# Two interleaved passes on one core: the rows, counts and rounds of the neighbour skipping take other places, and some operands move from SBUF to PSUM

## The chip, the cores and the metric

One Trainium2 chip, of which the program uses one core. A core has TensorE (matmuls and transposes, written to PSUM), VectorE (DVE), ScalarE (ACT), GpSimd (POOL) and SyncE (SP, which here only issues DMAs). Each works through its own queue in order and waits for the others by semaphores. The metric is the device time of one execution in microseconds, median of several runs.

## The reference, cut to what matters

Two layers on 16 graphs of 1024 nodes with 128 features and a 0/1 adjacency. Layer 0 is a gated graph network of four steps, then a residual and a normalization. Layer 1 first thins out the adjacency (the "skipping"), row after row, and then runs three aggregation layers on it.

```python
# layer 0, four steps
hw = einsum('bnc,cd->bnd', h, weight[i]);  m = einsum('bjn,bjd->bnd', adj, hw)
h = gru_cell(m, h, w_ih[i], w_hh[i], b_ih[i], b_hh[i])
...
# layer 1, the skipping: one step for each row n, in order
row = take(carry, n);  num = sum(row)
sf = where(num > 10, (num + 1) // 2, 1)
rank = cumsum(row)
rm = row & (rank % sf == 0)          # and only if num > 1 and the node is valid
carry[n] = row & ~rm;  carry[:, n] &= ~rm
```

A removal in a row also takes the entry out of that column, so later rows depend on earlier ones.

## The kernel before, in words

The program has two parts. The first, which the change touches, runs two passes side by side: class `Gated` (layer 0) and class `FixPoint` (the skipping). The second, `sage_layers`, is not touched. The order on every engine of the first part is the order in which the code issues instructions: nothing is reordered there, except in the preparation of the weights ahead of it.

**Gated.** Two streams, each with one graph at a time, take turns: for each pair of graphs and each step l from 0 to 3, one layer for stream 0 (s=0, called layer A here), then one for stream 1 (layer B). A layer is `layer(st, l, aside)`. Its 32 matmuls L1024 multiply the node features by the adjacency. The features are split into `h_hi` (rounded) and `h_lo` (the rest), and each part takes 16 matmuls over eight blocks `h_a` of the adjacency. Two ScalarE copies (L1029) bring the result to `h_ms`. Then come, for each half f of the nodes, six gate matmuls L1038 into the three `h_g` buffers, with a sigmoid (L1047), two VectorE operations (L1049, L1051), a tanh (L1052), a second sigmoid (L1055), and the new state: `h_zh` on GpSimd (L1057), `h_r` on VectorE (L1058), `h_h` on GpSimd (L1059).

While one stream computes, the other is made ready in callbacks `aside(n)`: `next_layer(f)` transposes the new state (L978, into the single PSUM buffer `h_tr`) and splits it; ScalarE writes `h_hi` (L968) and a copy `h_w` (L970), and GpSimd subtracts to get `h_lo` (L971). Around l=0, when a graph ends, `finish` adds the result to `h_x` and stores it to `e_sum` (L1010), `load_x` and `load_adj` load the next graph, `begin_rows` splits its features and `begin` transposes them (L990) into the state. Loads of `h_x` and stores of `e_sum` are issued by SP, loads of `h_a` by POOL.

**FixPoint.** A round treats rows k*128 to k*128+127 of G=4 graphs; k goes from 0 to 7 for each group of four graphs, so there are 32 rounds. The generator `steps` has 20 pieces for a round, each ended by `yield`. `aside` takes one piece at each call, and one more at the end of a layer, so a round lasts two layers, ten pieces in each. Layers A of a round have s=0, and since there are four steps l, rounds with k=0 and k=4 have l=0.

A round has these steps. `turn(i, g)` transposes the removals of earlier rows into the single PSUM buffer `f_tr` (L725, from `f_rt`, read back from memory, and from `f_nr`, the rows of the round before). `count` multiplies them into the row block `f_a` (L732) and scans it to `f_rank`, the running count (L734). `params` makes the divisors `f_q` (L699 to L703). `diag_u` (ScalarE, L856), `removed` (L863) and `less` (matmuls L871 into `f_pd`) solve the 128 x 128 diagonal block in two rounds of a fixed point; `f_both` (L795) marks the pairs in it that are present in both directions, from `f_low` (GpSimd, L767) and its transpose (L782). `wide_u` (ScalarE, L879 and L882) and the rows `end(g)` (L834) then give the block's removals `f_nr` for all columns; `end(g)` also stores them to `e_nr`, loads the `f_a` that is six row blocks on, and multiplies `f_s` on GpSimd (L840). `end(4)` adds up a check (L828, L830).

Before the change, the pieces stood so: layer A: rows 2 and 3; check; turn and count 0 with turns and counts 1, 2, 3 after them; transposes of `f_low`; `read_back` of the next round's `f_rt`. Layer B: `params`, `f_both`, `removed`, `less`, `removed`, `less`, `wide_u` of four graphs, rows 0 and 1.

Of the kernel before, what the change touches and what calls it, by code (L numbers as in the profile page):

```python
# [630 lines left out]
class FixPoint:  # L631
# [96 lines left out]
    def count(self, i, g, a, rank):  # L728
        nc = self.nc
        k, b0 = self.todo[i]  # L730
        if k:
            nc.vector.tensor_mul(a[:, :k * P], a[:, :k * P], self.pt[:, :k, :].rearrange("p k n -> p (k n)"))  # L732
        start = self.first[:, k, b0 + g:b0 + g + 1]
        nc.vector.tensor_tensor_scan(rank[:, g, 1:N + 1], self.zero.to_broadcast([P, N]), a,  # L734
                                     start, op0=ALU.add, op1=ALU.add)

    def steps(self):

        nc, G = self.nc, self.G
        for c in range(self.LOTS):  # L740
            self.load(c)
        end = None
        for i, (k, b0) in enumerate(self.todo):
            n0 = k * P
            diag = slice(n0, n0 + P)
            after = slice(n0 + 1, n0 + 1 + P)
            a = [self.loaded.pop((i, g)) for g in range(G // 2)]
            rank = self.two.tile([P, G, N + 2], F16, name="f_rank")

            if end:  # L750
                end(2)
                end(3)
            a += [self.loaded.pop((i, g)) for g in range(G // 2, G)]
            yield

            if end:
                end(4)
            nc.vector.tensor_copy(rank[:, :, 0], self.first[:, k, b0:b0 + G])
            yield

            self.turn(i, 0)
            self.count(i, 0, a[0], rank)
            yield
            self.turn(i, 1)
            low = self.small.tile([P, G, P], BF, name="f_low")
            for g in range(G):
                nc.gpsimd.affine_select(low[:, g, :], a[g][:, diag], pattern=[[-1, P]],  # L767
                                        compare_op=ALU.is_gt, fill=0.0, base=0, channel_multiplier=1)
            yield
            self.count(i, 1, a[1], rank)  # L770
            yield
            self.turn(i, 2)
            self.count(i, 2, a[2], rank)
            yield
            yield
            self.turn(i, 3)
            self.count(i, 3, a[3], rank)
            yield

            pt = self.ps.tile([P, G, P], BF, name="f_pd")  # L780
            for g in range(G):
                nc.tensor.transpose(pt[:, g, :], low[:, g, :], self.cst["ident_b"])  # L782
            yield

            for g in range(G):
                self.read_back(i + 1, g)
            yield

            q = self.params(rank[:, :, N])
            u = self.diag_u(rank[:, :, after], q)  # L790
            yield

            both = self.small.tile([P, G, P], BF, name="f_both")
            for g in range(G):
                nc.vector.tensor_mul(both[:, g, :], a[g][:, diag], pt[:, g, :])  # L795
            yield
            x = self.removed(u, q, both)
            yield

            yield  # L800
            rd = self.small.tile([P, G, P], F16, name="f_rd")
            pd, num = self.less(x, rank)
            q = self.params(num)
            nc.vector.tensor_sub(rd, rank[:, :, after], pd)
            u = self.diag_u(rd, q)
            yield

            yield
            x = self.removed(u, q, both)
            yield  # L810

            pd, num = self.less(x, rank)
            q = self.params(num)
            if k + 1 < NB:

                dn = self.small.tile([P, G], F32, name="f_dn")
                nc.vector.tensor_mul(dn, pd[:, :, P - 1], q[:, 0, :])
                nc.vector.tensor_sub(q[:, 3, :], q[:, 1, :], dn)
            nc.vector.tensor_sub(rank[:, :, after], rank[:, :, after], pd)
            us = {}  # L820
            self.wide_u(k, 0, us, rank, q)
            self.wide_u(k, 1, us, rank, q)
            yield
            s = self.small.tile([P, G, P], BF, name="f_s")

            def end(g, i=i, k=k, b0=b0, n0=n0, diag=diag, us=us, q=q, a=a, s=s, x=x, both=both):
                if g == G:
                    nc.gpsimd.tensor_tensor(s, s, x, ALU.add)  # L828
                    junk = self.small.tile([P, G, P], F16, name="f_ud")
                    nc.vector.scalar_tensor_tensor(junk, s, 1.0, both, op0=ALU.mult, op1=ALU.not_equal,  # L830
                                                   accum_out=self.bad[:, i:i + 1])
                    return
                nr = self.wide.tile([P, N], BF, name="f_nr", bufs=5)
                nc.vector.scalar_tensor_tensor(nr, us[g], q[:, 2, g:g + 1], a[g],  # L834
                                               op0=ALU.not_equal, op1=ALU.is_ge)
                nc.sync.dma_start(self.not_r[b0 + g, n0:n0 + P, :], nr)
                self.fresh[g] = nr
                self.load(G * i + g + self.LOTS)

                nc.gpsimd.tensor_tensor(s[:, g, :], nr[:, diag], both[:, g, :], ALU.mult)  # L840


            end(0)
            self.wide_u(k, 2, us, rank, q)
            self.wide_u(k, 3, us, rank, q)
            yield

            end(1)
            yield
        for g in range(2, G + 1):  # L850
            end(g)

    def diag_u(self, rd, q):
        u = self.small.tile([P, self.G, P], F16, name="f_ud")
        for g in range(self.G):
# [31 lines left out]
class Gated:  # L887
# [56 lines left out]
    class Stream:  # L944
# [14 lines left out]
        def load_x(self, b):  # L959
            if b < B:  # L960
                self.x[b] = self.top.wk.tile([P, NB, C], F32, name="h_x", bufs=3)
                self.nc.sync.dma_start(self.x[b], rows_of(self.top.x[b]))

        def split(self, f, src, whole):

            nc = self.nc
            rows = slice(4 * f, 4 * f + 4)
            nc.scalar.copy(self.hi[:, rows, :], src)  # L968
            if whole is not src:
                nc.scalar.copy(whole, src)  # L970
            nc.gpsimd.tensor_tensor(self.lo[:, rows, :], whole, self.hi[:, rows, :].bitcast(F32), ALU.subtract)  # L971

# [8 lines left out]
        def next_layer(self, f):  # L981
            self.split(f, self.turn(f), self.top.wk.tile([P, 4, P], F32, name="h_w"))

# [9 lines left out]
        def begin_rows(self, b):  # L993
            x = self.x[b]
            for f in range(2):
                rows = slice(4 * f, 4 * f + 4)
                self.split(f, x[:, rows, :], x[:, rows, :])

        def finish(self, f):
# [9 lines left out]
            if f == 1:  # L1009
                nc.sync.dma_start(rows_of(self.top.summed[b]), self.x.pop(b))  # L1010

    def layer(self, st, l, aside):
# [5 lines left out]
        for part in (st.hi, st.lo):  # L1018
            for j in range(NB):
                if j % 4 == 0:  # L1020
                    aside(n)
                    n += 1
                for f in range(2):
                    nc.tensor.matmul(pm[f], part[:, j, :], st.adj[j][:, half[f]],  # L1024
# [16 lines left out]
        for f in range(2):  # L1041
# [4 lines left out]
            pr = gate((w(self.wh, 0), h), (w(self.wi, 0), m))  # L1046
            nc.scalar.activation(r, pr, AF.Sigmoid, bias=bias(self.bs, 0))  # L1047
            ph = gate((w(self.wh, 2), h))
            nc.vector.scalar_tensor_tensor(r, ph, bias(self.bh, 2), r, op0=ALU.add, op1=ALU.mult)  # L1049
            px = gate((w(self.wi, 2), m))  # L1050
            nc.vector.tensor_add(r, px, r)  # L1051
            nc.scalar.activation(r, r, AF.Tanh, bias=bias(self.bi, 2))  # L1052
            aside(5 if f == 0 else 7)
            pz = gate((w(self.wh, 1), h), (w(self.wi, 1), m))
# [4 lines left out]
            nc.gpsimd.tensor_tensor(h, zh, r, ALU.subtract)  # L1059
            aside(6 if f == 0 else 8)  # L1060

    def run(self, steps):
# [7 lines left out]
        first.begin_rows(first.b)  # L1070
        for f in range(2):
            first.begin(f)
        for b0 in range(0, B, 2):
# [10 lines left out]
    def beside(self, ot, l, s, b0, steps):  # L1084
# [3 lines left out]
        if before in (0, L0):  # L1088
            old = not (s == 0 and b0 == 0)
            new = not (s == 1 and b0 + 2 >= B)  # L1090
            jobs = {5: [], 6: [], 7: [], 8: []}
            nxt = ot.b + 2 if old else ot.b
# [5 lines left out]
            if old:  # L1098
                jobs[5].append(lambda: ot.finish(0))
                jobs[6].append(lambda: ot.finish(1))  # L1100
                jobs[0] = [lambda: ot.load_x(nxt)]
                for j in range(NB):
                    jobs.setdefault(j // 2, []).append(lambda j=j: ot.load_adj(nxt, j))
            if new:
                jobs.setdefault(3 if old else 0, []).append(lambda: ot.begin_rows(nxt))
                jobs[7].append(begin)
                jobs[8].append(lambda: ot.begin(1))
        else:
            jobs = {5: [lambda: ot.next_layer(0)], 6: [lambda: ot.next_layer(1)]}

        def aside(n):
            next(steps, None)
            for job in jobs.get(n, ()):
                job()
            if n == 8:
                next(steps, None)
        return aside
# [90 lines left out]
```

## Time and profile before

| what | us |
|---|---|
| median of 3 runs (lowest to highest) | 3901.48 (3900.77 to 3902.44) |
| the profiled execution | 3903.16 |
| its span, first to last instruction | 3901.4 |
| VectorE busy in the span | 2743.0 (70%) |
| TensorE busy in the span | 2968.1 (76%) |
| GpSimd busy in the span | 1221.2 (31%) |
| last L834 of the first part starts | 1978.9 |

The page lists busy time by engine, the span in 40 slices, DMA queues, the chain of waits that ended last, the costliest groups of instructions and the DMA issues. In a line of a group or of the timeline, `out<-in` names the tiles; a bracket or the part behind the last bar gives the idle time of the engine ahead of it and what ended that. A duration under `xN` in the timeline spans N instructions.

### The profile page before, as it was taken

What the parts mean: (1) busy time and instruction counts of PE and PEld (TensorE: products, weight loads), DVE (VectorE), ACT (ScalarE), POOL (GpSimd) and SP (SyncE); (2) the same over time, 40 slices, a digit from 0 to 9 for tenths busy, and PEclk for the clock granted to TensorE, in tenths of its full rate; (3) what the DMA queues carried; (4) which work ended last, traced back from release to release, by engine and by line L of the source; (5) the groups of instructions that cost most, each with busy time, mean ns of one, the idle gap of its engine ahead of it and who ended that gap; (6) DMA issues with size and microseconds to landing.
All of it is one profiled execution on the core that took longest, in us unless ns stands there. A gap on an engine that the chain in (4) does not pass through costs nothing. (4 is left out here: it accounts for less than half of the span.)

```text
span 3901.4 us, 29884 instructions
## 1 busy us (share of the span) xinstructions
PE 2968.1 (76%) x9457; PEld 1604.6 (41%) x9457; DVE 2743.0 (70%) x4205; ACT 1149.9 (29%) x2006; POOL 1221.2 (31%) x1031
## 2 busy tenths in 40 slices
PE   5777767777677776767756867778687999899954
PEld 3444434444344443444433434434343444344422
DVE  3776767767677676766768888888885555455688
ACT  2443444434444443444321011010111333222221
POOL 2554455544555455554511001010100222122200
PEclk9898888988888888888877878888788999999976
DMA  4233232322324223242255656565564777576623
GB/s 149 69 118 103 78 135 69 129 93 79 135 69 141 80 79 135 69 159 63 63 174 188 210 172 221 172 211 205 178 209 174 245 240 243 191 243 238 221 76 98
DMA packets 305769, 577.76 MB, mean 148 GB/s; under 512 B 61057, under 2 KB 164258, under 8 KB 305602
## 3 DMA queue, kind: packets, MB, share of 16 engines
q1 hardware_dynamic: 287170, 508.64, 39.2%
q0 software_dynamic: 18432, 67.12, 4.7%
q8 instruction: 77, 1.26, 0.1%
q14 instruction: 90, 0.74, 0.1%
HBM read 449.79 MB, written 125.89 MB: 148 GB/s over the span
## 5 line engine op out<-in xcount | busy, mean ns | idle before, releaser
L455 POOL TENSOR_TENSOR s_os<-s_os,s_mf 128x512 f32<-128x512 f32 x96 | 121.7, 1267 | 1253.3 <-issue 1034.4
L1038 PE MATMUL h_g<-h_ms,h_wi 128*128 128x512 f32 x768 | 405.3, 610 | 120.1 <-ACT h_ms L1029 120.1
L434 PE MATMUL s_a<-b_at,s_t 128*128 128x512 f32 x1024 | 453.4, 593 | 0.0
L1038 PE MATMUL h_g<-h_h,h_wh 128*128 128x512 f32 x768 | 413.5, 621 | 10.4 <-ACT h_r L1047 10.4
L734 DVE TENSOR_TENSOR_SCAN f_rank<-f_zero,f_first,f_a 128x1024 f16<-128x1024 f32 x128 | 325.0, 2541 | 31.3 <-DMA f_a<-in_adj_dram 27.3
L454 DVE RECIPROCAL s_sq<-s_sq 128x512 f32<-128x512 f32 x96 | 321.0, 3344 | 33.4 <-ACT s_sq L453 33.4
L528 PE MATMUL a_pe<-ident,a_a 128*128 128x128 f32 x1024 | 177.6, 324 | 216.8 <-DVE a_a L523 114.8
L1057 POOL TENSOR_TENSOR h_zh<-h_z,h_h 128x512 f32<-128x512 f32 x128 | 250.0, 1953 | 258.2 <-ACT h_z L1055 258.2
L1024 PE MATMUL h_m<-h_a,h_lo 128*128 128x512 f32 x1024 | 325.3, 477 | 0.0
L1058 DVE SCALAR_TENSOR_TENSOR h_r<-h_z,h_r 128x512 f32<-128x512 f32 x128 | 171.0, 1336 | 191.3 <-ACT h_z L1055 191.1
L971 POOL TENSOR_TENSOR h_lo<-h_w,h_hi 128x512 fp32r<-128x512 f32 x96 | 146.4, 1525 | 487.7 <-ACT h_w L970 487.7
L434 PEld LDWEIGHTS s_a<-b_at,s_t 128*128 128x128 f32 x1024 | 195.1, 191 | 246.0 <-issue 245.8
L535 PE MATMUL s_o<-a_at,ones 128*128 128x512 f32 x512 | 265.0, 666 | 21.5 <-DVE a_at L529 21.5
L1038 PEld LDWEIGHTS h_g<-h_ms,h_wi 128*128 128x128 f32 x768 | 149.1, 196 | 316.7 <-issue 170.5
L1049 DVE SCALAR_TENSOR_TENSOR h_r<-h_g,h_bh,h_r 128x512 f32<-128x512 f32 x128 | 95.7, 747 | 260.0 <-PE h_g L1038 170.9
L1024 PE MATMUL h_m<-h_a,h_hi 128*128 128x512 f32 x1024 | 266.2, 414 | 0.0
L528 PEld LDWEIGHTS a_pe<-ident,a_a 128*128 128x128 f32 x1024 | 146.8, 169 | 287.4 <-issue 209.9
L1024 PEld LDWEIGHTS h_m<-h_a,h_lo 128*128 128x128 f32 x1024 | 235.5, 236 | 70.1 <-POOL f_low L767 18.9
L834 DVE SCALAR_TENSOR_TENSOR f_nr<-f_u,f_q,f_a 128x1024 bf16<-128x1024 f16 x128 | 232.0, 1870 | 0.0
L434 PE MATMUL s_a<-a_at,a_s 128*128 128x512 f32 x512 | 230.2, 592 | 0.0
L1024 PEld LDWEIGHTS h_m<-h_a,h_hi 128*128 128x128 f32 x1024 | 195.7, 194 | 50.9 <-issue 11.5
L1059 POOL TENSOR_TENSOR h_h<-h_zh,h_r 128x512 f32<-128x512 f32 x128 | 191.1, 1493 | 31.2 <-DVE f_q L700 23.0
(153 smaller groups left out, 4942.8 us busy)
## 6 DMA issues: line engine op xcount, KB each, us to landing
b_at<-at SPq DMA_DIRECT2D x256, 512.0 KB, 4.4
h_a<-in_adj_dram POOLq DMA_DIRECT2D x128, 512.0 KB, 8.5
f_a<-in_adj_dram SPq DMA_DIRECT2D x128, 512.0 KB, 4.9
a_a<-in_adj_dram SPq DMA_DIRECT2D x128, 512.0 KB, 4.1
at<-a_at SPq DMA_DIRECT2D x32, 2048.0 KB, 8.8
e_nr<-f_nr SPq DMA_DIRECT2D x128, 256.0 KB, 3.7
a_nr<-e_nr SPq DMA_DIRECT2D x32, 1024.0 KB, 7.3
s_mf<-in_nodemask_dram SPq DMA_DIRECT2D x48, 512.0 KB, 4.3
```

The source lines that it names most:

```text
L434: nc.tensor.matmul(pa[f], rows[j // 4][:, j % 4, :], at[j][:, f * HF:(f + 1) * HF], start=(j == 0), stop=(j == NB - 1))
L454: nc.vector.reciprocal(sq, sq)
L528: nc.tensor.transpose(pe[:, i, :], a[:, j * P:(j + 1) * P], ident)
L535: nc.tensor.matmul(pd, ones, at[j][:, f * HF:(f + 1) * HF], start=(j == 0), stop=(j == NB - 1))
L734: nc.vector.tensor_tensor_scan(rank[:, g, 1:N + 1], self.zero.to_broadcast([P, N]), a, start, op0=ALU.add, op1=ALU.add)
L834: nc.vector.scalar_tensor_tensor(nr, us[g], q[:, 2, g:g + 1], a[g], op0=ALU.not_equal, op1=ALU.is_ge)
L971: nc.gpsimd.tensor_tensor(self.lo[:, rows, :], whole, self.hi[:, rows, :].bitcast(F32), ALU.subtract)
L1024: nc.tensor.matmul(pm[f], part[:, j, :], st.adj[j][:, half[f]], start=(j == 0 and part is st.hi), stop=(j == NB - 1 and part is st.lo))
L1038: nc.tensor.matmul(pg, lhs, rhs, start=(i == 0), stop=(i == len(mm) - 1))
L1057: nc.gpsimd.tensor_tensor(zh, z, h, ALU.mult)
L1058: nc.vector.scalar_tensor_tensor(r, z, 1.0, r, op0=ALU.subtract, op1=ALU.mult)
L1059: nc.gpsimd.tensor_tensor(h, zh, r, ALU.subtract)
```

## The change: what it does

*Rows.* `end(0)` to `end(3)` move to the first four pieces of the next round, so to the places between the 32 matmuls of layer A. `wide_u` of the fourth graph follows `end(0)` (`more`). The other three come in the last piece of layer B.

*Counts and turns.* Each turn and each count has a piece of its own: turn and count 0, turn 1, count 1 between the gates of layer A; turn 2, count 2, turn 3 (with `read_back`), count 3 between the 32 matmuls of layer B. The check moves from the second piece to the last of layer A. The solution of the diagonal block follows in layer B from the start of its gates.

*Operands.* The scan takes the row block as first operand and, instead of a column of zeros in SBUF, a column of the PSUM buffer `f_tr`, whose value it ignores (op1 is bypass). `diag_u` writes to PSUM in float32 (name `f_pd`, one buffer, shared with `less` and the diagonals' transposes). The diagonals are transposed in float32 right out of `f_a`, and one GpSimd select on `f_both` takes the place of four on `f_low`. `h_lo` of a next layer is subtracted on VectorE out of `h_tr` (`rest`), without the copy `h_w`; only `begin_rows` still subtracts on GpSimd, from `h_x` itself.

*Places and queues in Gated.* There is a tenth call of `aside`, behind the second half's first sigmoid, so that the places run from 0 to 9, and no double step at the end. `next_layer` and `rest` take places 5 to 8. `begin(1)` moves into the stream's own first layer, ahead of the third of its four groups of matmuls. Loads of `h_x` and stores of `e_sum` are issued by POOL.

```diff
     def count(self, i, g, a, rank):
...
+        out, start = rank[:, g, 1:N + 1], self.first[:, k, b0 + g:b0 + g + 1]
         if k:
...
-        nc.vector.tensor_tensor_scan(rank[:, g, 1:N + 1], self.zero.to_broadcast([P, N]), a,
-                                     start, op0=ALU.add, op1=ALU.add)
+            nc.vector.tensor_tensor_scan(out, a, pt[:, 0, 0:1].to_broadcast([P, N]), start,
+                                         op0=ALU.add, op1=ALU.bypass)
+        else:
+            nc.vector.tensor_tensor_scan(out, a, self.zero.to_broadcast([P, N]), start,
+                                         op0=ALU.add, op1=ALU.add)
...
+            for g in range(G):
+                if end:
+                    end(g)
+                    if g == 0:
+                        more()
+                yield
+            a = [self.loaded.pop((i, g)) for g in range(G)]
             rank = self.two.tile([P, G, N + 2], F16, name="f_rank")
...
             nc.vector.tensor_copy(rank[:, :, 0], self.first[:, k, b0:b0 + G])
+            pt = self.ps.tile([P, G, P], F32, name="f_pd")
+            for g in range(G):
+                nc.tensor.transpose(pt[:, g, :], a[g][:, diag], self.cst["ident"])
             yield
 
             self.turn(i, 0)
             self.count(i, 0, a[0], rank)
             yield
...
             for g in range(G):
                 nc.vector.tensor_mul(both[:, g, :], a[g][:, diag], pt[:, g, :])
+            nc.gpsimd.affine_select(both, both, pattern=[[0, G], [1, P]], compare_op=ALU.is_gt, fill=0.0,
+                                    base=0, channel_multiplier=-1)
+            yield
+            self.turn(i, 1)
+            yield
+            self.count(i, 1, a[1], rank)
+            yield
+            if end:
+                end(G)
+            yield
+            self.turn(i, 2)
+            yield
+            self.count(i, 2, a[2], rank)
+            yield
+            self.turn(i, 3)
+            for g in range(G):
+                self.read_back(i + 1, g)
+            yield
+            self.count(i, 3, a[3], rank)
+            yield
...
     def diag_u(self, rd, q):
-        u = self.small.tile([P, self.G, P], F16, name="f_ud")
+        u = self.ps.tile([P, self.G, P], F32, name="f_pd")
...
-                self.nc.sync.dma_start(self.x[b], rows_of(self.top.x[b]))
+                self.nc.gpsimd.dma_start(self.x[b], rows_of(self.top.x[b]))
...
+    def rest(self, f):
             rows = slice(4 * f, 4 * f + 4)
+            self.nc.vector.tensor_sub(self.lo[:, rows, :], self.src, self.hi[:, rows, :].bitcast(F32))
...
-                nc.sync.dma_start(rows_of(self.top.summed[b]), self.x.pop(b))
+                nc.gpsimd.dma_start(rows_of(self.top.summed[b]), self.x.pop(b))
...
                     aside(n)
                     n += 1
+                    if n == 3 and l == 0:
+                        st.begin(1)
...
+            if f == 1:
+                aside(7)
...
-            aside(5 if f == 0 else 7)
+            aside(5 if f == 0 else 8)
...
-            aside(6 if f == 0 else 8)
+            aside(6 if f == 0 else 9)
...
-            jobs = {5: [lambda: ot.next_layer(0)], 6: [lambda: ot.next_layer(1)]}
+            jobs = {5: [lambda: ot.next_layer(0)], 6: [lambda: ot.rest(0)],
+                    7: [lambda: ot.next_layer(1)], 8: [lambda: ot.rest(1)]}
```

## The prediction

> **What bounds the kernel now.** The page's slices show POOL busy in the first half only: the changed part, "the two passes", is the first 1985 us. The chain of waits holds lines of the later stages only, so I read this part round by round. A round of the skipping is two layers: A (stream 0) and B (stream 1). First the windows answer (us, then busy PE, PEld, DVE, ACT, POOL, then the granted clock): one round from the last L871 of one to that of the next, and the whole steady part.
>
> ```profile
> 1797.40:1853.66 56.26, 44.38 (x161) 26.55 (x160) 42.76 (x62) 23.29 (x40) 27.16 (x21) 0.91 0.21 68
> 112.00:1928.00 1816.00, 1336.31 (x4749) 790.26 (x4750) 1284.81 (x1791) 745.73 (x1331) 920.53 (x781) 0.88 0.31 100
> ```
>
> No engine is full. TensorE has most work and stops in layer A twice each round, and the clock falls after each stop (timeline, PE and DVE):
>
> ```profile
> 1799.93 0.68 DVE L819 TENSOR_TENSOR f_rank<-f_rank,f_pd 128x512 f16<-128x512 f16 x1
> 1804.80 7.23 DVE L834 SCALAR_TENSOR_TENSOR f_nr<-f_u,f_q,f_a 128x1024 bf16<-128x1024 f16 x4
> 1807.14 0.29 PE L725 MATMUL f_tr<-ident_b,f_nr 128*128 128x128 bf16 x1 [3.69 <-DVE f_nr L834]
> 1807.19 3.40 PE L1024 MATMUL h_m<-h_a,h_lo 128*128 128x512 f32 x8
> ...
> 1815.66 0.58 PE L725 MATMUL f_tr<-ident_b,f_rt 128*128 128x128 bf16 x4 [5.07 <-DMA f_a<-in_adj_dram]
> 1832.32 3.91 PE L1024 MATMUL h_m<-h_a,h_hi 128*128 128x512 f32 x16
> ```
>
> The first stop waits for the first new row block f_nr. The second is put down to a DMA long done; the single `f_tr` buffer is what it needs, free at L732 (1814.8), behind four L834 and the L830 junk operation. Eight L1024 then take 3.4 us where sixteen take 3.9. So the round is 41.1 us of matmuls, about 12 of idle TensorE, 3.4 of half clock.
>
> VectorE's own durations are stretched beside GpSimd: four L863 take 1.29 us alone, 4.22 beside L971 and L1057.
>
> ```profile
> 1839.03 1.29 DVE L863 SCALAR_TENSOR_TENSOR f_x<-f_ud,f_q,f_both 128x128 bf16<-128x128 f16 x4
> 1849.51 4.22 DVE L863 SCALAR_TENSOR_TENSOR f_x<-f_ud,f_q,f_both 128x128 bf16<-128x128 f16 x4
> L734 DVE TENSOR_TENSOR_SCAN f_rank<-f_zero,f_first,f_a 128x1024 f16<-128x1024 f32 x128 | 325.0, 2541 | 31.3 <-DMA f_a<-in_adj_dram 27.3
> L971 POOL TENSOR_TENSOR h_lo<-h_w,h_hi 128x512 fp32r<-128x512 f32 x96 | 146.4, 1525 | 487.7 <-ACT h_w L970 487.7
> ```
>
> Rounds are not alike. L758 starts each: 55.2 us apart in rounds with l=1 and 2, 60.2 over l=3, and 70.6 over l=0:
>
> ```profile
> 292.15 0.29 DVE L758 CAST f_rank<-f_first 128x4 f16<-128x4 f32 x1
> 306.82 0.62 ACT L968 CAST h_hi<-h_x 128x512 fp32r<-128x512 f32 x1 [21.21 <-DMA h_x<-in_x_dram]
> 309.84 2.07 PE L1038 MATMUL h_g<-h_ms,h_wi 128*128 128x512 f32 x2 [11.39 <-ACT h_ms L1029]
> 362.79 0.25 DVE L758 CAST f_rank<-f_first 128x4 f16<-128x4 f32 x1
> ```
>
> The load of h_x, issued at 289.4, lands 17 us later behind f_a and h_a; ScalarE waits in order, so h_ms and the gates wait too. This comes seven times. Last, the start:
>
> ```profile
> 35.57 0.90 PE L927 MATMUL h_tr<-ident,h_w_in 128*128 128x128 f32 x3 [28.50 <-DVE h_wi L928]
> ```
>
> A scan (L734) stands ahead of L928 on VectorE and waits for its rows until 32.7; the first L1024 starts at 63.0.
>
> [...]granted 0.50 from 1807 to 1810, after 3.69 us idle. [...]I leave the scan's time as it is when op1 becomes bypass.
>
> **The change, part by part.** Each layer still has ten places. I walk one round (k=5), zero at layer A's first gate matmul, with durations of the trace: gate matmul 0.86, a place of L1024 1.9, turn 0.5, four transposes of h 0.6, count 3.15 (mult 0.8, scan 2.35), PSUM operations of 512 elements 0.7, matmul end to reader 0.27.
>
> *Rows (L834), now in A's first four places, no longer between matmuls.* No L1024 waits for them: the 3.69 and 5.07 us stops go. But the third and fourth row load of the next round are issued after the first and second f_nr, and the new f32 transposes of the diagonals read those rows ahead of A's gates. From B's gates (zero there): L819 ends at 17.2; ScalarE's three f_u follow at 1.43 each; f_nr one 20.2, f_nr two 22.6 (1.22 each, h_h L1059 between). Load issued at 23.05, landing after 3.9 (f_a: 3.3 least, 4.9 median): 27. L1024 ends at about 23.6. TensorE idles some 3 us, and the gates, ScalarE's sigmoid and VectorE's L1049 queue behind it. The f32 transposes take 0.6 for L782's 0.39. The four f_rt loads move to B's third place: they wait on SP for turn 3, ahead of nothing but the next e_nr (16 us later), and are read a layer later: nothing.
>
> *Counts.* The scan now reads one SBUF operand and a PSUM column of `f_tr`, so the next turn waits for the scan, not for the mult. In A: L1051 4.4, count 7.5, L1058 9.1 (held by zh), four `both` 10.0, the new DVE subtraction `rest(0)` 10.7. Only then is `h_tr` free: the second transposes wait 2.2 us. Count 1 ends at 17.1; turn 2, ready at 14.8, waits 2.3. Junk waits for h_h and the f_s sum (1.15), ends at 21.8; count 2 ends at 24.9; turn 3, ready at 21.3, waits 3.6. Count 3 and the parameters end where B's L1024 do.
>
> *`f_ud` to PSUM, one affine for four.* L863 reads one SBUF operand: 1.3 each time, 2.9 less in B. Each of the four activations now waits for the one before: about +0.5, twice. Four POOL selects (1.48) become one of 512 elements (not in the trace: 1.15 from the L828 row to 2.3; off the path, its result is due a layer later). In B the first L871 waits 0.7, the second transposes 2.2 for `rest(0)`.
>
> *Split.* 96 ScalarE copies (0.59) and 96 POOL L971 (1.53) go, 96 DVE subtractions of 0.7 come; counted above.
>
> Sum of a normal round: matmuls 41.4, idle 3.0 + 2.2 + 2.3 + 3.6 + 0.7 + 2.2 + 1.0 = 15.0, half clock after the two gaps over 3 us (1.7 each, at 0.7 chance) 2.4: 58.8, **2.5 us worse** than 56.26. With k=0 there are no turns: 4 us less.
>
> *h_x on POOL's queue.* It is issued behind the first f_s and ahead of h_a; on POOL it stands behind no SP row load. Issue about 22, landing 27 to 29 (h_a's median is 8.5, f_a's 4.9): at most 3 us past the rows, less 1.5 since finish needs no `rest`. Round l=0: +1.5 over normal, against +14.3 now. The e_sum store, too, only follows on POOL. Round l=3: begin(1) leaves the end of B, where L990 waited 4.1 for ScalarE behind f_u, for A's third place: -1 against +4.7.
>
> Eight rounds: k=1,2,5,6 4 x 2.5 = +10; k=3,7 2 x (2.5 - 4.7 - 1) = -6.4; k=4 2.5 - 14.3 + 1.5 = -10.3; k=0 -14.3. Sum -21, four times -84; the first round has no h_x stop (+12.8), the last l=3 no load (+3.7): -67.5.
>
> *Start.* The scan leaves L928's front. All loads of the start (24 of 512 KB, 1.8 MB of weights) are 14.4 MB, 46 us at the 315 GB/s seen while rows load; h_x stands ninth on POOL's queue, the last weights behind six row loads. First L1024 at about 43, between the weights' arrival and the last load: -20 (bounds 0 and -30). *End.* All four f_nr follow the last layer, beside finish: +2.
>
> Sum -85.5 from the profiled execution's 3903.16 us (span 3901.4 and 1.8 around): 3817.7. It lies 1.7 above the median of 3901.48, so I say **3817**. A measurement here can tell 0.2%, 8 us, from no change.
>
> **Rivals.** *Rows land in time:* landing 3.3 and f_nr back to back take away the 3.0 and about 1.0 of half clock in 30 rounds: 3697. For it: L834 of 1.22 between POOL operations; against: 1.5 MB in 4.8 us at 315 GB/s. [...]then 2.9 us stay in B, 30 times 87: 3905, no change. Against: it is short whenever POOL rests. *Slower: the rows in front of the gates.* One mechanism, at the diagonal transposes. Each us of landing costs a us in 30 rounds; it decides from 85.5 / 30 = 2.9 us beyond my 3.9, 6.8 us. At h_a's 8.5 the sum is 30 x 4.6 = +138: 3955. For it: store and load of 0.75 MB per f_nr are queued together; against: f_a's 4.9 median today, with the same stores. *The change does not do what it says* is met by the second case. [...] Slower by 0.2 us, +18.
>
> **How the numbers follow.** Forecast 0.46 (own range 3775 to 3865, from +-1.3 us a round); rows in time or fast scan 0.16; partway between forecast and no change 0.05; no change 0.05; slower 0.28, since a walk leaves out waits more easily than it invents them. Faster 0.66, same 0.06, slower 0.28. The range 3735 to 3925 leaves out one in ten at each end.
>
> **What would show it.** Right: pitch of l=1 rounds near 58, of l=0 near 60; no wait over 5 us of h_hi for h_x; L863 near 0.33 us; new waits of f_pd for f_a (3 us), of f_tr for the scan (2.3 and 3.6), of h_tr for the DVE subtraction (2.2); first L1024 near 43. Wrong: f_pd for f_a above 6.8 us, a granted clock below 0.85, or L834 longer than 1.9.

## The result, and the profile after

The kernel after takes **3915.38 us** (median of 4, 3914.64 to 3915.82), the kernel before 3901.18 beside it: ratio 1.0036, 95% interval 1.0018 to 1.0053. It is slower by about 14 us, where 84 us less were forecast. The profiled execution has a span of 3913.8 us against 3901.4.

Line numbers of the kernel after, where they differ: rows f_nr L833, product L734, scan L736 (L739 for k=0), rank copy L761, transposes of the diagonal L764, removal L858, `less` L866, transposes of h L973, rest L966, adjacency matmuls L1023, gates L1037, h_zh L1058, h_h L1060, h_hi of a new graph L992, load of h_x L957, copies to h_ms L1028.

First the windows answer (columns as before: us, then busy PE, PEld, DVE, ACT, POOL, then the granted clock), for one round from the last L866 of one round to that of the next, and for the steady part. The round has k=6 (its product L734 below runs over 768 columns); the one that the prediction shows of before has k=5:

```profile
399.79:459.12 59.33, 44.22 (x166) 26.09 (x164) 39.95 (x64) 21.52 (x36) 18.27 (x14) 0.94 0.21 67
112.00:1928.00 1816.00, 1372.50 (x4711) 803.88 (x4710) 1155.09 (x1870) 682.50 (x1202) 693.62 (x612) 0.90 0.29 98
```

VectorE, ScalarE and GpSimd all have less to do than before (1155 us for 1285, 682 for 746, 694 for 921), and the clock is no lower. Yet this round is 3 us longer than the round of before in the prediction, which lasts 56.26 us, and 4 us longer than before's mean for k=6 (55.9). Work was taken off engines that were not full; what counts is where TensorE stops. This is the timeline of that round, its stops in layer A:

```profile
404.35 6.50 DVE L833 SCALAR_TENSOR_TENSOR f_nr<-f_u,f_q,f_a 128x1024 bf16<-128x1024 f16 x4 [0.71 <-ACT f_u L877]
413.31 0.33 PE L764 MATMUL f_pd<-ident,f_a 128*128 128x128 f32 x1 [3.12 <-DMA f_a<-in_adj_dram]
425.42 0.63 PE L973 MATMUL h_tr<-ident,h_h 128*128 128x128 f32 x4 [1.97 <-POOL h_h L1060]
431.95 0.44 PE L725 MATMUL f_tr<-ident_b,f_rt 128*128 128x128 bf16 x5 [2.47 <-DVE f_rank L736]
439.70 0.44 PE L725 MATMUL f_tr<-ident_b,f_rt 128*128 128x128 bf16 x5 [3.53 <-DVE f_rank L736]
```

The two stops of before (3.69 for f_nr, 5.07 for `f_tr`) are gone, and four new ones stand there: a late row (3.12), `h_tr` (1.97; put down to h_h, but the h_h that it reads was ready at 407.0, and it starts 0.14 us behind the end of L966, so the buffer is what it needed), and two turns that wait for the scan. These four are close to the forecast's 3.0, 2.2, 2.3 and 3.6. The surprise stands in layer B, all engines in order of time:

```profile
450.79 1.77 POOL L1058 TENSOR_TENSOR h_zh<-h_z,h_h 128x512 f32<-128x512 f32 x1 [15.22 <-ACT h_z L1056]
451.54 1.04 DVE L699 SCALAR_TENSOR_TENSOR f_t<-f_num,f_const 128x4 f32<-128x4 f32 x1
452.63 1.26 POOL L1060 TENSOR_TENSOR h_h<-h_zh,h_r 128x512 f32<-128x512 f32 x1
452.68 1.23 DVE L701 SCALAR_TENSOR_TENSOR f_t<-f_t,f_q 128x4 f32<-128x4 f32 x1
454.70 0.68 DVE L966 TENSOR_TENSOR h_lo<-h_tr,h_hi 128x512 fp32r<-128x512 f32 x1
455.53 1.09 PE L973 MATMUL h_tr<-ident,h_h 128*128 128x128 f32 x4 [3.39 <-DVE h_lo L966]
456.40 1.91 PE L1037 MATMUL h_g<-h_h,h_wh 128*128 128x512 f32 x2
```

L699 works on four columns, takes 0.16 us where no GpSimd operation runs beside it, and here ends when GpSimd's L1058 ends; L701 ends with L1060 in the same way. The rest L966 is queued behind both, TensorE's transposes wait for the rest for 3.39 us, and the next two gates run at half clock (granted 0.50 from 454.99 to 458.40; 1.91 us, e15 below shows them at 1.02).

The groups (busy us, mean ns of one, idle time before):

```profile
L736 DVE TENSOR_TENSOR_SCAN f_rank<-f_a,f_first,f_tr 128x1024 f16<-128x1024 f32 x112 | 263.2, 2350 | 4.0
L858 DVE SCALAR_TENSOR_TENSOR f_x<-f_pd,f_q,f_both 128x128 bf16<-128x128 f32 x256 | 71.8, 343 | 52.0 <-ACT f_pd L851 52.0
```

So the operand moves did what they say: the scan is at 2350 ns wherever it runs (2348 to 2352 in 112 places; before, 2541 on average and 2320 to 3160), the removal at 343 (340 to 352; before, 730 and 337 to 1423). TensorE's waits in the first 2000 us (total us, times, longest) show what took their place:

```profile
PE f_tr L725 <- DVE f_rank L736: 148.2, 56, 3.9
PE f_pd L764 <- DMA f_a<-in_adj_dram: 92.6, 49, 3.9
PE h_tr L973 <- DVE h_lo L966: 82.2, 25, 3.4
PE h_tr L973 <- POOL h_h L1060: 49.7, 23, 2.4
```

Last an l=0 round. The load of h_x is issued on GpSimd's queue and lands 7 us later; ScalarE and then TensorE wait for it, and the gate matmuls after the stop run at half clock (granted 0.50 from 291.15 to 297.98; two of them take 2.08 us):

```profile
283.39 0.94 POOL L957 DMA_DIRECT2D h_x<-in_x_dram  x1
290.57 1.14 ACT L992 CAST h_hi<-h_x 128x512 fp32r<-128x512 f32 x2 [6.00 <-DMA h_x<-in_x_dram]
292.25 2.08 PE L1037 MATMUL h_g<-h_ms,h_wi 128*128 128x512 f32 x2 [2.53 <-ACT h_ms L1028]
```

The pitch of the rounds, from rank copy to rank copy (mean over the rounds with the same k, the first round left out, us):

| k (l of layer A) | before | after | change | forecast |
|---|---|---|---|---|
| 0 (l=0) | 70.93 | 60.59 | -10.3 | -14.3 |
| 1, 2 | 54.77 | 60.39 | +5.6 | +2.5 |
| 3 (l=3) | 59.48 | 59.61 | +0.1 | -3.2 |
| 4 (l=0) | 70.42 | 62.51 | -7.9 | -10.3 |
| 5, 6 | 56.32 | 60.69 | +4.4 | +2.5 |
| 7 (l=3) | 61.41 | 62.09 | +0.7 | -3.2 |

### The profile page after: what moved, and what is told of

It is laid out like the page before. It is cut to its first block, busy times and chain, and to the rows that moved or that the text cites. A ratio compares the mean times of both kernels' runs of the same rounds, so it can differ in the third digit from the quotient of the medians.

```text
span 3913.8 us, 29541 instructions
## 1 busy us (share of the span) xinstructions
PE 3018.7 (77%) x9457; PEld 1626.0 (42%) x9457; DVE 2623.8 (67%) x4301; ACT 1088.6 (28%) x1878; POOL 1003.0 (26%) x871
## 5 line engine op out<-in xcount | busy, mean ns | idle before, releaser
L1037 PE MATMUL h_g<-h_h,h_wh 128*128 128x512 f32 x768 | 457.0, 680 | 17.4 <-ACT h_r L1046 17.4
L1037 PE MATMUL h_g<-h_ms,h_wi 128*128 128x512 f32 x768 | 445.3, 665 | 17.7 <-ACT h_ms L1028 17.7
L1058 POOL TENSOR_TENSOR h_zh<-h_z,h_h 128x512 f32<-128x512 f32 x128 | 193.4, 1511 | 966.7 <-ACT h_z L1056 966.5
L1023 PE MATMUL h_m<-h_a,h_lo 128*128 128x512 f32 x1024 | 285.7, 438 | 0.0
L1023 PE MATMUL h_m<-h_a,h_hi 128*128 128x512 f32 x1024 | 267.4, 415 | 0.0
L1037 PEld LDWEIGHTS h_g<-h_ms,h_wi 128*128 128x128 f32 x768 | 165.8, 217 | 241.1 <-issue 189.7
L736 DVE TENSOR_TENSOR_SCAN f_rank<-f_a,f_first,f_tr 128x1024 f16<-128x1024 f32 x112 | 263.2, 2350 | 4.0
L1023 PEld LDWEIGHTS h_m<-h_a,h_lo 128*128 128x128 f32 x1024 | 217.6, 216 | 61.2 <-issue 12.9
L1023 PEld LDWEIGHTS h_m<-h_a,h_hi 128*128 128x128 f32 x1024 | 196.8, 195 | 59.7 <-issue 20.2
L833 DVE SCALAR_TENSOR_TENSOR f_nr<-f_u,f_q,f_a 128x1024 bf16<-128x1024 f16 x128 | 206.9, 1673 | 14.5 <-ACT f_u L877 12.1
L1060 POOL TENSOR_TENSOR h_h<-h_zh,h_r 128x512 f32<-128x512 f32 x128 | 193.2, 1509 | 67.1 <-DVE h_r L1059 61.1
L529 DVE TENSOR_TENSOR a_at<-a_pe,a_nr 128x512 f32<-128x512 f32 x256 | 164.9, 680 | 44.8 <-PE a_pe L528 44.7
L447 ACT ACTIVATE s_sq<-s_o,vt 128x512 f32<-128x512 f32 x96 | 65.4, 682 | 452.3 <-PE s_o L443 451.3
```

The costliest lines, as they stand in the source:

```text
L529: nc.vector.tensor_mul(at4[f][:, :, k * P:(k + 1) * P], pe, nr[f][:, :, k * P:(k + 1) * P])
L736: nc.vector.tensor_tensor_scan(out, a, pt[:, 0, 0:1].to_broadcast([P, N]), start, op0=ALU.add, op1=ALU.bypass)
L1037: nc.tensor.matmul(pg, lhs, rhs, start=(i == 0), stop=(i == len(mm) - 1))
L1058: nc.gpsimd.tensor_tensor(zh, z, h, ALU.mult)
```

## The experiments

Seventeen kernels ran. Each time below is a median; kernels that ran side by side share their runs of before (3901.6 to 3902.9 us), so a kernel is compared with another through its ratio to before.

### Late rows: e1, e11

e1 is the kernel after with

```
-    LOTS = 6
+    LOTS = 8
```

and, for room in SBUF, the weights' load tile laid into the tile h_zh and one buffer for f_s and f_rd.

> The kernel after with eight row buffers instead of six, so that every row of a round is loaded one round ahead. (Room for them: the weights' load tile of the start lies in another tile, f_s and f_rd have one buffer instead of two.) Theory 'late rows': the diagonal transposes no longer wait for a row (3.1 to 3.9 us in each of 49 waits of the kernel after), and the half clock that follows (1.7 us) goes too: 3 to 4.7 us a round, 90 to 150 us over 32 rounds less what the next wait takes back, so 3770 to 3830 us. Rival 'VectorE sets the round': the wait moves on to the turns and the time stays within 15 us of 3915. Rival 'the clock alone': the wait goes, the clock falls by as much, 3900 or more.

Measured: **3820.54**, ratio 0.9802 (0.9776 to 0.9828). The wait of L764 is gone from TensorE's list; the wait for the scan is unchanged:

```profile
PE f_tr L725 <- DVE f_rank L736: 149.2, 56, 3.8
```

The clock of the steady part stays at 0.90, so the clock alone is ruled out. Rounds with l=1 and 2 fall from 60.4 to 54.5 us on average (k=1, 2), 5.9 each; l=0 rounds do not fall at all (61.0 and 63.6), which led to e7. The late row was worth 91 us by the ratios, 95 by the medians.

e11 gives the kernel before eight row buffers and h_x on GpSimd (its yardstick, with six buffers, is e3; room for them is made as in e1, from a few tiles more).

> The kernel before with x and its store on GpSimd (3833 us as it stands) and eight row buffers. Theory 'rows were in time in the old order, since the diagonal was transposed after the fourth turn': 3815 to 3840 us, 20 us less at most (its trace shows 32 us of waits for rows). Rival 'rows are late in any order': 60 to 100 us less, 3735 to 3775.

Measured: 3836.18, ratio 0.9830 (0.9815 to 0.9846), against 0.9830 for e3. In the old order, more row buffers bring nothing. So the 95 us are a cost of the new order, in which six buffers are too few. That order both issues the row loads later and reads the rows earlier, by the transposes of the diagonal ahead of the gates; which of the two weighs more was not tried.

### h_x on GpSimd's queue: e3, e4, e7

e3 makes only this edit in the kernel before, e4 takes only this back in the kernel after:

```
-    self.nc.sync.dma_start(self.x[b], rows_of(self.top.x[b]))
+    self.nc.gpsimd.dma_start(self.x[b], rows_of(self.top.x[b]))
...
-    nc.sync.dma_start(rows_of(self.top.summed[b]), self.x.pop(b))
+    nc.gpsimd.dma_start(rows_of(self.top.summed[b]), self.x.pop(b))
```

> The kernel before with one edit of the change alone: the load of x and the store of its sum are issued by GpSimd, not SyncE. Theory 'the gain of the l=0 rounds came from this': seven l=0 rounds lose about 10 us each and the start about 10, so 3810 to 3835 us, faster than both kernels. Rival 'it came from the earlier place of finish and begin, and the queue matters little': within 15 us of 3901. Rival 'GpSimd waits for the sum in front of its store and its loads of adjacency come late': 3905 to 3930.

> The reverse of the run before: the kernel after with the load of x and its store back on SyncE. Theory: the wait of h_hi for h_x returns in the l=0 rounds, 7 to 10 us in each of seven, and at the start some 10 more: 3970 to 3990 us. Rival 'the queue matters little': within 15 us of 3915.

Measured: e3 **3833.52**, ratio 0.9830 (0.9813 to 0.9846); its l=0 rounds fall from 70.9 and 70.4 to 58.4 and 57.0 us. e4 3889.95, ratio 0.9972 (0.9957 to 0.9986): taking the edit back makes the kernel after faster, against this run's theory and its rival. The l=0 rounds fall to 58.2 and 58.3, and ScalarE's wait for h_x from 135.2 us in 15 places to 40.6 in 8. In e4 the load on SyncE's queue lands in 5 us, where GpSimd's took 7:

```profile
291.34 0.40 SPq L957 DMA_DIRECT2D h_x<-in_x_dram  x1
296.35 1.14 ACT L992 CAST h_hi<-h_x 128x512 fp32r<-128x512 f32 x2 [2.32 <-DMA h_x<-in_x_dram]
```

The same edit gains 68 us in the old order and costs about 25 in the new one. In the old order SyncE's load of h_x had a median of 26.9 us from issue to landing, GpSimd's in e3 7.1. In the trace of before, four row stores and four row loads stand on SyncE's queue from 283.6 us on, and h_x follows at 289.4. In e4 one store and one load stand ahead of it (290.4 to 291.2). So little is left for the other queue to avoid, and the issue costs GpSimd 0.94 us where SyncE takes 0.40. That this is why the gain turns round is argued from the order of issue; it was not tried alone.

e7 joins e1 and e4.

> Eight row buffers (as in the run that had 3820) and the load of x with its store back on SyncE (as in the run that had 3890). Theory 'the two are separate': the l=0 rounds fall from 61.0 and 63.6 to about 58 us, the others stay near 55, so 3790 to 3800 us. Rival 'with more rows on SyncE's queue x comes late': 3815 to 3840.

Measured: **3755.21** (3746.6 to 3767.7), ratio 0.9614 (0.9598 to 0.9630). The l=0 rounds are 55.2 and 55.0 us, near the 54.6 (k=1, 2) and 56.3 (k=5, 6) of normal rounds. The two edits bring more together than the sum of the two alone (160 for 95 and 25): the l=0 rounds do not fall with e1 alone and fall to 58 us with e4 alone, so there each edit is worth more with the other one.

### The scan's operand: e2, e8, e9

```
-    nc.vector.tensor_tensor_scan(out, a, pt[:, 0, 0:1].to_broadcast([P, N]), start, op0=ALU.add, op1=ALU.bypass)
+    nc.vector.tensor_tensor_scan(out, self.zero.to_broadcast([P, N]), a, start, op0=ALU.add, op1=ALU.add)
```

> The kernel after with the scan as it was before (its zeros are a column in SBUF, not one of f_tr), so that f_tr is free when the product is done, 2.35 us earlier in each turn. Theory 'f_tr is held through the scan': the waits of the turns fall from 2.5 and 3.5 us by up to 2.35 each, 3 to 4.7 us a round in 28 rounds, 80 to 130 us, so 3785 to 3835 us; ahead of that goes a scan of 2.5 instead of 2.35 us. Rival 'VectorE's order sets the turns': the product itself is late, the waits stay, 3905 to 3925 us. [...]

> Eight row buffers and the scan of before. With the six-buffer kernel the scan of before brought 13 us, not the 80 to 130 expected. Theory 'it was small because the late rows stood ahead of the turns': with the rows in time the same edit brings more, 30 to 80 us, so 3740 to 3790. Rival 'VectorE's product is the wait of turn 2 and 3 anyway': again about 13 us or less, 3800 to 3820.

> The three edits together: eight row buffers, x and its store on SyncE, the scan of before. Theory 'each takes away its own wait': 3755 less the 39 us that the scan brought once the rows were in time, so 3705 to 3730 us. Rival 'in the l=0 rounds only one of them can be had': 3730 to 3755. Rival 'VectorE or the weight loads are the bound now': 3750 or more.

Measured: e2 3902.43, ratio 1.0003 (0.9996 to 1.0010), 13 us less than after; e8 **3781.41**, ratio 0.9691 (0.9674 to 0.9707), 39 to 43 less than e1; e9 3742.68, ratio 0.9594 (0.9580 to 0.9609), 8 to 13 less than e7. Waits for the product stand in place of waits for the scan (99.7 us in 32 places in e9, for 144.0 in 56 in e7). The edit is worth a gain, always smaller than the 4.7 us a round that its waits seemed to promise: the next turn waits for the product instead. That e8 gains more than e9 may be the spread between executions: in the profiled ones the gains are 38 and 29 us. This is left open.

### The stretched removal: e5

e5 is the kernel before with f_ud as the tile f_pd in PSUM.

> The kernel before with diag_u written to PSUM (the f_pd bank) instead of SBUF, and nothing else. [...]the removal on VectorE (L863, mean 730 ns) falls to about 340 ns a group of 128 columns, and what waits for it on TensorE (f_pd from f_x, 46 to 53 us in all) rises or falls by under 20 us, because the four activations now wait for the bank to be read and write 1.95 instead of 1.65 us; time 3885 to 3910. Rival 'it was the place in the round': L863 stays above 600 ns, time the same as before within 8 us.

Measured: 3897.65, ratio 0.9987 (0.9981 to 0.9994), about 5 us less. The group of the removal:

```profile
L863 DVE SCALAR_TENSOR_TENSOR f_x<-f_pd,f_q,f_both 128x128 bf16<-128x128 f32 x256 | 71.6, 340 | 64.5 <-ACT f_pd L856 64.5
```

In the old order, with this one tile moved (and so written in float32), 730 ns become 340, which is what the removals of before took where no GpSimd operation ran beside them (345 ns in 135 places, against 1160 in the 121 others). So the stretch came with f_ud as a second SBUF operand. But 104 us of VectorE's time bring 5 us. TensorE's waits for the removal tell why, first before, then in e5:

```profile
PE f_pd L871 <- DVE f_x L863: 46.4, 79, 1.0
PE f_pd L871 <- DVE f_x L863: 66.3, 32, 2.6
```

Before, TensorE waited 46 us for the removal in all, so not much more than that could come back. And e5 brings a wait of its own: ScalarE's f_ud now needs the bank of `f_pd`, which is free only behind L795 (in the first pass it waits 181 us for L795, where before it waited 153 for L702), so the removal of the first pass starts later. The 5 us are what is left of a gain and a loss. In the new order the removal's operand was not moved back.

### What holds h_tr: e6, e10, e12, e13, e14, e15

e6 puts the old split back (ScalarE copies twice, GpSimd subtracts); e13 keeps the rest on VectorE but emits it ahead of the fixed point's step:

```
         def aside(n):
+            if before not in (0, L0) and n in (6, 8):
+                jobs[n].pop()()
             next(steps, None)
```

> The kernel after with the split of the new rows as it was before: ScalarE copies the turned rows to SBUF a second time and GpSimd subtracts, so that h_tr is free after ScalarE. Theory 'h_tr is held through VectorE's rest': the 48 waits of the h_tr transposes (132 us in all) fall to under 1 us each and the half clock after them goes, 40 to 90 us in all, so 3825 to 3875 us. Rival 'GpSimd and the second copy take it back' (GpSimd's subtraction beside VectorE's small operations, h_lo late for the next layer's second half): 3900 to 3930. Rival 'the next wait takes it': the waits for f_x or f_rank grow by as much, 3905 to 3920.

> The kernel after, in which the rest of the split (VectorE, 0.68 us) is emitted ahead of the fixed point's step at the same point of the gates, not behind it. Theory 'VectorE's order keeps h_tr': the 48 waits of the h_tr transposes (132 us in all) fall below 1 us each; each step of the fixed point starts 0.7 us later, which the waits for f_x may show; 30 to 80 us less than 3915, so 3835 to 3885. Rival 'as with the split of before, f_x takes it': about 24 us less, 3885 to 3895, with the wait for f_x at 150 us or more. Rival 'the rest itself waits for ScalarE's h_hi': the waits stay, within 10 us of 3915.

Measured: e6 3891.32, ratio 0.9972 (0.9961 to 0.9983); e13 3874.42, ratio 0.9925 (0.9909 to 0.9942). In both, the wait of h_tr falls (in e6 it leaves the list), and the wait for f_x grows from 53 us. TensorE's waits in e13:

```profile
PE f_pd L866 <- DVE f_x L858: 135.8, 61, 4.9
PE h_tr L973 <- DVE h_lo L966: 32.7, 24, 1.6
```

So who frees h_tr, and when, is worth about 25 us (e6) and 42 (e13), but the wait moves on to f_x: something ahead of both the rest and f_x is late. The candidates are the small operations of `params`. e12 writes three of the five with constants in the instruction:

```
-        stt(t[:, 0, :], num, 0.25 + 2.0 ** -14, halves, op0=ALU.mult, op1=ALU.add)
+        nc.vector.tensor_scalar(t[:, 0, :], num, 0.25 + 2.0 ** -14, HALVES, op0=ALU.mult, op1=ALU.add)
```

> The kernel after with three of the five small operations of params written with one operand in SBUF and constants in the instruction (tensor_scalar), where they read a second operand of constants from SBUF. Theory 'two SBUF operands beside GpSimd are held': L699 falls from 616 to about 160 ns in its 64 places, L701, which keeps its two, stays at 518 ns, the waits of h_tr for VectorE in the second stream fall by 0.5 to 1 us, and the time by 10 to 35 us, 3880 to 3905. Rival 'any VectorE operation there is held': L699 stays above 500 ns and the time within 8 us of 3915. Rival 'the next one is held instead': L699 falls, L701 grows by as much.

Measured: 3917.61, ratio 1.0040 (1.0027 to 1.0054), no change. With one SBUF operand in this form L699 is held as it was with two (616 ns in the kernel after):

```profile
L701 DVE SCALAR_TENSOR_TENSOR f_t<-f_t,f_q 128x4 f32<-128x4 f32 x96 | 49.6, 517 | 3.3
L699 DVE TENSOR_SCALAR f_t<-f_num 128x4 f32<-128x4 f32 x64 | 39.8, 622 | 2.2
```

The expectation took it that a single SBUF operand is not held; for `tensor_scalar` the 622 ns speak against that. Why is not shown by any run here.

e15 takes the holding away by giving each operation of the second pass one PSUM operand, in used-up columns of f_pd:

```
             pd, num = self.less(x, rank)
-            q = self.params(num)
             nc.vector.tensor_sub(rd, rank[:, :, after], pd)
+            nc.vector.tensor_sub(pd[:, :, 0], rank[:, :, N], pd[:, :, P - 1])
+            q = self.params(num, pd[:, :, 1:3].rearrange("p g t -> p t g"), pd[:, :, 0])
```

with the first two operations of `params` reading that copy of num, and its intermediate values t in those columns. The subtraction for `rd` moves ahead of `params`, but both stay ahead of the rest.

> The kernel after, in which the params of the second pass (one of three sets a round) read one operand from PSUM in each operation: the number and the two intermediate values lie in columns of f_pd that are used up; one subtraction more. Theory 'the holding until GpSimd's instruction ends costs 2.0 us a round in the second stream': L699 and L701 of this set fall from 1.04 and 1.23 to about 0.2 us each, the wait of h_tr for VectorE from 3.4 to about 1.5 us, the half clock behind it goes, and the time falls by 40 to 90 us, 3825 to 3875. Rival 'f_x is then waited for, as when the split of before was put back': 0 to 25 us less, 3890 to 3915.

Measured: **3832.71**, ratio 0.9824 (0.9808 to 0.9841), 83 us less than after; the clock of the steady part rises from 0.90 to 0.92. The same place in layer B (lines of the file one or two higher than after: L700 is after's L699, L968 its L966, L975 its L973, L1039 its L1037, L1062 its L1060):

```profile
438.81 0.17 DVE L700 SCALAR_TENSOR_TENSOR f_pd<-f_pd,f_const 128x4 f32<-128x4 f32 x1
439.11 1.27 POOL L1062 TENSOR_TENSOR h_h<-h_zh,h_r 128x512 f32<-128x512 f32 x1
439.22 0.17 DVE L702 SCALAR_TENSOR_TENSOR f_pd<-f_pd,f_q 128x4 f32<-128x4 f32 x1
439.56 0.68 DVE L968 TENSOR_TENSOR h_lo<-h_tr,h_hi 128x512 fp32r<-128x512 f32 x1
440.39 0.63 PE L975 MATMUL h_tr<-ident,h_h 128*128 128x128 f32 x4 [1.78 <-POOL h_h L1062]
440.86 1.02 PE L1039 MATMUL h_g<-h_h,h_wh 128*128 128x512 f32 x2
```

Beside GpSimd's h_h, L702 takes 0.17 us instead of 1.23; the rest follows; TensorE waits 1.78 instead of 3.39, and the pair of gates after it takes 1.02 us instead of 1.91. So the holding is what the 83 us were paid for: operations of the same size in the same places, held in one kernel and not in the other.

e10 and e14 try the old split and the rest ahead of the step on top of e9.

> The three edits and the split of before (ScalarE's second copy, GpSimd's subtraction), which took all h_tr waits away in the kernel after but gave most of it to longer waits for f_x (53 to 176 us). Theory 'the removal on VectorE comes late because its params are held by GpSimd's subtraction': the exchange stays the same, 10 to 40 us less than without, 3670 to 3720 us. Rival 'with the other waits gone the late f_x is all that is left': no gain or up to 20 us more than without, 3720 to 3745.

> The fastest kernel so far (eight row buffers, x and its store on SyncE, the scan of before; 3743 us) with the rest ahead of the step. Theory 'the waits are separate': 30 to 80 us less, 3660 to 3715. Rival 'VectorE's chain sets the rest of the round, as when the split of before was added': 3730 to 3755.

Measured: e10 3745.21, ratio 0.9592 (0.9578 to 0.9607), no gain; its wait for f_x is 175.5 us in 61 places. e14 3723.11, ratio 0.9537 (0.9517 to 0.9557), 20 us less than e9. With the small operations held, going round them is worth 0 to 22 us there.

### All together: e16, e17

> Eight row buffers, x and its store on SyncE, the scan of before, and the params of the second pass with one operand in PSUM. If the terms are separate: 3743 less 83, 3645 to 3675 us. Rival 'VectorE or the waits of the turns take it': 3700 to 3745.

> The same with the rest ahead of the fixed point's step. If h_tr still waits for VectorE about 2 us in each stream: 10 to 30 us less than the run beside it. Rival: with the small operations no longer held, the rest is not late, and putting it ahead only delays f_x: 0 to 20 us more.

Measured: e16 **3655.19** (3653.3 to 3657.3), ratio 0.9362 (0.9345 to 0.9379), 6.4% faster than before and the fastest of all; e17 3658.22, ratio 0.9369 (0.9352 to 0.9386), no gain from the order once the second pass's `params` are not held. e16 is the kernel after with eight row buffers, h_x and its store on SyncE, the scan of before and e15's `params`. Its rounds with k=1 and 2 are 50.1 us, and the clock of its steady part is 0.94:

```profile
112.00:1680.00 1568.00, 1291.15 (x4709) 776.33 (x4708) 1135.67 (x1899) 685.56 (x1204) 705.16 (x585) 0.94 0.34 113
```

## Why the prediction was wrong

It forecast -85.5 us for the profiled execution; it came to +12.4. Term by term, from the pitches: the 16 rounds with k=1, 2, 5, 6 are 2.5 us each above the forecast (40 us), the 7 with l=3 about 3.5 (25), the four with k=4 2.4 and the three later ones with k=0 4.0 (22), the start and first round 8, the end 3. The sum is the 98 us by which it failed. Nearly all of it is an excess of 2.4 to 4 us in every round.

In the 16 rounds with k=1, 2, 5, 6, measured between rank copies, TensorE is idle for 14.7 us on average, and 15.0 were forecast. That the idle sum fits is luck: the second h_tr wait in B is 1.2 us longer than forecast, the rows 0.4, the turns are 0.6 shorter, and the 1.0 for the four activations shows as no idle time of its own. The matmuls take 45.8 us where 43.8 were forecast, 41.4 and a half clock of 2.4. This is 2.0 of the 2.5 us. The last 0.7 is the round that was walked: it lasted 56.26 us, but the mean of these rounds before is 55.5.

- **The step that failed: "the second transposes 2.2 for `rest(0)`" in layer B, and the half clock "after the two gaps over 3 us" that was counted without it.** The place and the mechanism (h_tr freed by VectorE) were right, the sizes were not: the wait is 3.4 us, so it is a third gap over 3 us, and gates at half clock follow it (granted 0.50). The walk took the small operations of `params` at their undisturbed 0.16 us; two of them are held by GpSimd and take 1.04 and 1.23 us. The holding beside GpSimd had been read off the profile for the removal (4.22 us against 1.29), and this term was not asked for it. e15, which takes this holding away, gains 83 us, 2.6 a round on average. In the 16 rounds above, TensorE's idle time falls by 1.3 us and the matmuls' by 1.9, to 43.9, which is the forecast. Before, L701 was held too, in 32 places, but ahead of the first pass, where the rest was on GpSimd and h_tr was freed by ScalarE, so nobody waited:

```profile
1836.74 1.29 POOL L1059 TENSOR_TENSOR h_h<-h_zh,h_r 128x512 f32<-128x512 f32 x1 [0.72 <-DVE f_q L700]
1836.75 1.30 DVE L701 SCALAR_TENSOR_TENSOR f_t<-f_t,f_q 128x4 f32<-128x4 f32 x1
```

  The change put the rest on the queue behind the held operations. The limit of 3 us, which the trace of before did not show, was too high as well. Before, each of the 46 falls of the clock between 112 and 1928 us came behind a stop of 3.57 us or more. In the kernel after there are 84, and in 23 of them no stop of the 6 us ahead reached 3.0 us. Which shorter stops bring it and which do not was not worked out.
- **Late rows, right in kind and size.** Forecast 3.0 us a round and about 1 of half clock; the trace shows 3.12 in the round shown and 92.6 in 49 waits, and e1 gained 95 us. It was rightly in the sum. The rival *rows land in time* priced its absence at 120 us, and e1 confirms that within a quarter. The *slower* rival is not what happened: its sign was a wait of f_pd for f_a above 6.8 us, and the longest wait of L764 is 3.9.
- **Turns behind the scan, right as waits, smaller in worth.** 2.3 and 3.6 were forecast, 2.47 and 3.53 are in the timeline. Adding them in full was too simple: with the old operand the same turns wait for the product, and 8 to 43 us come back, not 4.7 a round.
- **The removal's 2.9 us in B.** The duration fell as forecast (343 ns), but in the old order it brings 5 us in all (e5), not 87, and TensorE's waits for the removal were 46. That the stretch goes with the second SBUF operand was not shown when it was forecast; e5 shows it (730 ns with it, 340 without). The rival in which the 2.9 us stay gave about the measured total by luck.
- **h_x.** The wait over 5 us that was to be gone is there (6.0 in the round shown), and the l=0 rounds are 60.6 and 62.5 us, near the 60 forecast, all the same. The forecast credited the queue, so this is luck: in the new order the queue costs about 25 us (e4), and the gain of these rounds comes from the new order itself.
- **l=3.** Forecast -1 against a normal round; measured -0.8 (k=3, against k=1 and 2) and +1.4 (k=7, against k=5 and 6). `begin` at A's third place does free the end of B: the wait of its transposes for ScalarE falls from 4.1 and 3.3 us to 1.3 and 0.4. But a wait for the removal of 5.4 us a round stands there now, which was 1.5 before, and most of it is one stop behind the same held operations (here with k=3):

```profile
273.12 0.61 PE L866 MATMUL f_pd<-f_tri,f_x 128*128 128x128 bf16 x4 [4.89 <-DVE f_x L858]
```

- **Start.** First adjacency matmul forecast at 43 us, measured at 52.2 (63.0 before): the scan no longer stands in front of the weights, and TensorE waits for a load of weights for the last time until 38.74. Behind it their preparation still takes 13 us, in which TensorE and VectorE take turns at the single buffer h_tr, and the transposes of h_x stand behind that:

```profile
38.74 0.87 PE L922 MATMUL h_tr<-ident,h_w_in 128*128 128x128 f32 x3 [2.50 <-DMA h_w_in<-in_L_gnn_w_ih_dram]
46.53 0.90 PE L922 MATMUL h_tr<-ident,h_w_in 128*128 128x128 f32 x3 [0.65 <-DVE h_wi L923]
52.23 5.51 PE L1023 MATMUL h_m<-h_a,h_hi 128*128 128x512 f32 x16
```

- **A slip of 1 us.** 3817.7 less 1.7 is 3816, not 3817; it changes nothing.

## What to carry to other kernels

Before work is moved to an engine, look at what stands in front of it on that engine's queue and whether another engine can hold that: a 0.16 us operation that ends with GpSimd's 1.3 us one costs nothing where nobody waits behind it, and 2.6 us a round where a PSUM buffer is freed behind it. Ask of a stretched operation, small or large, who waits for its end before pricing the stretch, and move an operand to PSUM where somebody does (1.23 us became 0.17 in e15). Price the half clock behind a stop (1.91 us for two gates instead of 1.02, behind 3.39 us) together with the stop. Where a new order issues loads later or reads them earlier, count the buffers again (eight instead of six here), and try again a queue that helped in the old order.

## What was not expected of the hardware

A small VectorE instruction with two SBUF operands lasted until the GpSimd instruction beside it ended: L699 and L701, on 128x4 values, took 0.16 us alone, 1.04 and 1.23 beside two GpSimd operations, and ended within 0.1 us of their ends. In the kernel after, all 32 L701 that ran beside GpSimd's h_h took 1.23 us on average, the 64 others 0.16. L868, which reads one of its two operands from PSUM, took 0.15 us beside GpSimd's h_zh (32 places) as elsewhere. Taking the holding away also raised the granted clock of the steady part, from 0.90 to 0.92 in e15; in the fastest kernel, with the other edits, it is 0.94.
